# A two-layer graph transformer on one core: three tiles' q by rank kept on chip, row sums moved, and the last weight loads on another queue

## The chip, the cores and the metric

The kernel runs on one core of one Trainium2 chip. The time is the device time of one execution in microseconds. Of the kernel before there are three runs; their median is 1984.96 us (1980.67 to 1987.98). Besides, one execution was recorded by the hardware profiler.

TensorE (PE in the profile) multiplies matrices, VectorE (DVE), ScalarE (ACT) and GpSimd (POOL) work on rows, and SyncE (SP) only issues transfers. ScalarE and GpSimd issue transfers too. Each engine works through its own instructions in order; semaphores make one wait for another.

## The reference, cut to what matters

There are 2708 tokens of 512 numbers, 8 heads of 64, and two layers, each with its own weights. The graph is sparse: a token is joined to itself and to some others, at most 22 in the longest lists that the kernel plans for.

```
mask = adj + eye
q, k, v = h @ Wq.T + bq, h @ Wk.T + bk, h @ Wv.T + bv          # 8 heads of 64
scores = where(mask == 0, -1e9, q . k / sqrt(64))
ctx = softmax(scores) @ v
h1 = layer_norm(h + ctx @ Wo.T + bo, ln1)
h2 = layer_norm(h1 + relu(h1 @ W1.T + b1) @ W2.T + b2, ln2)     # W1: 2048 x 512
```

The second layer takes the first one's h2. Everything is float32.

## The kernel before, in words

`by_edges` works on edges. It sorts the tokens by the number of their neighbours ("by rank"), so that the 128 tokens of a tile have lists of about one length. There are 22 tiles; tile 21 has the shortest lists (3 entries at most) and only 20 tokens, tile 0 the longest (22). `order` is the order of work: tiles 21, 20, 19, 18, 8, 9, 7, 10 and so on, and two neighbours in it make a block (`blocks[0]` is 21 and 20, `blocks[1]` is 19 and 18).

**Keys and lists.** `first` projects k and v of all tokens in their given order and stores them in `kv_d` in DRAM; beside it VectorE reads the adjacency rows and finds each token's neighbours. `ranked` (line 735) then multiplies small matrices on TensorE (L742, L749), takes the ranks out of them on VectorE (L756 to L764), and GpSimd scatters each token's list to its rank (L768, 22 indirect transfers), reads all back (L779) and makes `ident_i`, the tokens in order of rank (L794). In the last two steps of the key phase `beside_keys` loads bias rows and the first weights; `load_second` adds two pairs of rows on VectorE (L1144), which stand in VectorE's order just ahead of L756.

**Queries.** `first_queries` (line 862) projects q of all tokens in their given order, two tiles at a time, into tiles `qs`, and stores them in `q_d` (`written`, L872 and L876). With tile t = `OWN` = 9 it begins on q by rank for the first four tiles of `order`: `own_rows` gathers the tokens' rows of x (two are asked for ahead of the loop, `xr`), `turned_own` transposes them on TensorE (L1100), `own_query` projects them. The first two q stay on chip. The other two are stored in `q_own` (L925) and loaded from there when attention asks for them (L971). All others are gathered from `q_d` by rank (L952), which can start when all of `q_d` is written.

**Attention.** `attend` is a generator. Each step takes one chunk of two list entries of a tile: GpSimd has gathered k and v of these neighbours (`loads`, L952, five buffers), VectorE multiplies by q (L991) and sums by head (L997), ScalarE takes exponentials (L1010) and weighs v (L1017), VectorE adds up (L1023, L1030). At the end of a tile `sums` and `divided` give the attended rows `cx` (L1061). `advance` takes steps as far as a credit allows, `through(k)` takes as many as block k needs. Attention's gathers of k, v and q stand on GpSimd's one queue.

**Feed-forward.** `attended` transposes `cx` (L1100, evicted at L1105), projects it by Wo (o, L568) and normalises (h, L1223 to L1094, with a reciprocal root on GpSimd, L1090). `turned` transposes h into `hT`. `feed_forward` (line 1240) runs over 16 slices f of W1: four matmuls `pf` (L1265), a relu on ScalarE (`ft`, L1273), and the second product `a` of three slices earlier (L1253). Three PSUM tiles hold `pf`, so that of slice f waits for the relu of slice f - 3. In the feed-forward of a block the next block's attention steps, its `attended` (at f = 10 and 11) and `turned` (after f = 15) are woven in.

For the first block `attended` is woven into the query loop: `beside_queries` (line 1417) transposes `cx` at t = NT - 7 = 15 and projects o at t = 16.

**Order.** TensorE, ScalarE and SyncE follow the order of the program. GpSimd does so up to the end of the query loop, VectorE in the query loop and at the start of layer 1; elsewhere a scheduler orders these two when the kernel is built.

**Weights.** W1 and W2 come in eight pieces each (`w1_0` to `w1_7`, `w2_0` to `w2_7`, 512 KB a piece). Pieces 5 to 7 lie in the buffers that the key and query loops use for x (`xg`) and for `kvs` and `qs`, so they can be loaded only after these loops. Lines 1439 to 1441 issue them on SyncE's queue behind the last stores of `q_d`:

```
for j in range(len(now.w1), NFC // 2):
    now.load_w1(j)
    now.load_w2(j)
```

Of the kernel before, what the change touches and what calls it, by code (L numbers as in the profile page):

```python
# [18 lines left out]
P = 128  # L19
DM = 512  # L20
# [22 lines left out]
XB, XBS = 256, 11  # L43
LEAD = 1.3
QT = 6
OWN = 9
EARLY = 3
PACE = (0.62, 0.72)

# [421 lines left out]
def by_edges(ctx: ExitStack, tc: tile.TileContext, x, xT, adj, layers, out, good):  # L471
# [30 lines left out]
    ps = ctx.enter_context(tc.tile_pool(name="ps", bufs=3, space=PSUM))  # L502

    own = {}
    at = None

    ident = const.tile([P, P], F32, name="ident")
# [10 lines left out]

    kv_d = [dram.tile([N, 2 * DM], F32, name=f"kv_d{n}") for n in range(NL)]
    q_d = [dram.tile([N, DM], F32, name=f"q_d{n}") for n in range(NL)]  # L520
    q_own = dram.tile([N, DM], F32, name="q_own")
# [340 lines left out]
    def first_queries(bq, wq, listed, pa, tokens, meanwhile):  # L862

        nonlocal at
        xrs = [own_rows(g) for g in blocks[0]]
        made = []

        def written():
            t, qs = made.pop(0)
            if t + 2 < NT:  # L870
                out = q_d[0][t * P : (t + 2) * P, :].rearrange("(two p) c -> p two c", p=P)
                nc.sync.dma_start(out=out, in_=qs)  # L872
                return
            for i in range(2):
                r = size(t + i)
                nc.sync.dma_start(out=q_d[0][(t + i) * P : (t + i) * P + r, :], in_=qs[:r, i])  # L876

        for t in range(NT):
            r = size(t)
            if t % 2 == 0 and made:  # L880
                written()
            q = project(tokens(t, 1), r, wq, "q", other=t % 2 > 0)
            if t % 2 == 0:
                qs = wts.tile([P, 2, DM], F32, tag=f"w2_{5 + t // 2 % 3}", name="qs")
                made.append((t, qs))
            nc.vector.scalar_tensor_tensor(
                qs[:r, t % 2], q[:r], DK**-0.5, bq[:r], ALU.mult, ALU.add
            )
            if t == OWN - 1:
                listed()  # L890
                pa.__exit__(None, None, None)
                at = ctx.enter_context(tc.tile_pool(name="at", bufs=2))
                for g in blocks[0]:
                    own[g] = at.tile([P, DM], F32, tag="q", name="q", bufs=QB)
                to = dict(own)
                next(ahead)
            if t in (OWN, OWN + 2):
                k = (t - OWN) // 2
                zTs = [turned_own(g, xr) for g, xr in zip(blocks[k], xrs)]
                for g, xr, zT in zip(blocks[k], xrs, zTs):  # L900
                    own_query(g, zT, to.get(g, xr), bq, wq)
                    advance(0.5)
                xrs = [own_rows(g) for g in blocks[1]] if k == 0 else []
            meanwhile(t)
        while made:
            written()

    def own_rows(g):
        r = size(g)
        xr = dn.tile([P, DM], F32, tag="row", name="xr", bufs=3)  # L910
        gather(xr[:r], x, ident_i[:r, g : g + 1])
        return xr
# [6 lines left out]
    def own_query(g, zT, to, bq, wq):  # L919

        r = size(g)
        q = project(lambda c: zT[:, c, :r], r, wq, "q")
        nc.vector.scalar_tensor_tensor(to[:r], q[:r], DK**-0.5, bq[:r], ALU.mult, ALU.add)
        if g in blocks[1]:
            nc.sync.dma_start(out=q_own[g * P : g * P + r, :], in_=to[:r])  # L925

    def checked():

# [32 lines left out]
    def asked(n, g):  # L961

        r = size(g)
        if g in own:
            return own.pop(g)
        q = at.tile([P, DM], F32, tag="q", name="q", bufs=QB)
        if n == 0 and g not in blocks[1]:
            gather(q[:r], q_d[0], ident_i[:r, g : g + 1])
        else:
            table = q_own if n == 0 else q_d[n]  # L970
            nc.sync.dma_start(out=q[:r], in_=table[g * P : g * P + r, :])  # L971
        return q

    def chunks_of(g):
# [134 lines left out]
    class Layer:  # L1109
# [27 lines left out]
        def load_second(self, part, temp):  # L1137

            w = self.w

            def sum_of(one, tag, other):
                t, u = row(w, one, tag), temp()
                nc.sync.dma_start(out=u, in_=other.to_broadcast([P, DM]))
                nc.vector.tensor_tensor(t, t, u, ALU.add)  # L1144
# [200 lines left out]
    def attend(n, got):  # L1345

        peak = small.tile([P, NT], F32, tag="peak", name="peak", bufs=1)
        nc.vector.memset(peak, 0.0)
        loaded = loads(n)
        steps = []  # L1350
        for g in order:
            cuts = chunks_of(g)
            steps += [(g, s0, c, i, i + 1 == len(cuts)) for i, (_, s0, c) in enumerate(cuts)]
            if g == order[1]:
                steps += [None] * 3
        steps += [None] * 3
        kv = next(loaded)
        yield 0.0
        q = asked(n, order[0])
        done = [None] * 3  # L1360
        for k, step in enumerate(steps):
            if step:
                g, s0, c, i, last = step
                if i == 0:
                    t = Tile(g, q)
                if k > 0:
                    kv = next(loaded)
                t.weights(kv, s0, c)
                if i == 1 and g != order[-1]:
                    q = asked(n, order[order.index(g) + 1])  # L1370
                done.append((t, kv, s0, c, last))
            else:
                done.append(None)
            t3, t2, t1 = done[-4:-1]
            if t1:
                t1[0].weigh(*t1[1:4])
            if t2 and t2[-1]:
                t2[0].sums(peak)
            if t3 and t3[-1]:
                got[t3[0].g] = t3[0].divided()  # L1380
# [22 lines left out]

    got = {}
    ahead = attend(0, got)
    early = {}

    def beside_keys(t):

        if t == NT - 5:  # L1410
            now.load_first()
        if t > NT - 3:
            now.load_second(t + 2 - NT, temp)
            now.load_w1(t + 2 - NT)
            now.load_w2(t + 2 - NT)

    def beside_queries(t):

        if len(now.w2) < 5:
            now.load_w1(len(now.w1), nc.scalar)  # L1420
            now.load_w2(len(now.w2), nc.scalar)
        if t > OWN:
            advance(1.0 if t < NT - 7 else 0.45)
        if t == NT - 7:
            through(0)
            early[0] = now.attended(blocks[0], got)
            next(early[0])
        if t == NT - 6:
            for _ in blocks[0]:
                next(early[0])  # L1430

# [3 lines left out]
    with tc.manual_schedule(engines={mybir.EngineType.Pool}):  # L1435
        made = first(layers[0], beside_keys)
        with tc.manual_schedule(engines={mybir.EngineType.DVE}):
            first_queries(*made, beside_queries)
    for j in range(len(now.w1), NFC // 2):
        now.load_w1(j)  # L1440
        now.load_w2(j)
    behind, pool = None, []
    for n in range(NL):
        last = n == NL - 1
# [23 lines left out]
        *_, hs = early[n]  # L1468
        hT = now.turned(blocks[0], hs)
        turning = projecting = None  # L1470
        for k, block in enumerate(blocks):
            more = k + 1 < NB
            asking = iter(())
# [2 lines left out]
            for f, zs in enumerate(now.feed_forward(block, hs, hT)):  # L1476
                if f == NFC:
                    break
                if f in (5, 6) and behind:
                    next(behind)  # L1480
                    if f == 6:
                        for _ in behind:
                            advance(1.0)
                        behind = None
                if more and f == 10:
                    through(k + 1)
                    projecting = now.attended(blocks[k + 1], got)
                    next(projecting)
                if more and f == 11:
                    for hs_next in projecting:  # L1490
                        advance(0.5 if k else 0.0)
                advance(PACE[n] if k else 1.1 if f < 10 else 0.4)
                if f in (0, 3, 7, 9):
                    next(asking, None)
                if more and f == NFC - 1:
                    finish(asking)
                    hT = now.turned(blocks[k + 1], hs_next)
                if n > 0 and (k, f) == (0, 2):
                    now.load_second(1, temp)
                if not last:  # L1500
# [14 lines left out]
                if not last and not more:  # L1515
# [7 lines left out]
                    if f == 7:  # L1523
                        finish(ahead)
                        pool += nxt.preloaded(order[:8], temp)
            if not last:
                behind = now.keys_values(block, zs)
            if more:
# [77 lines left out]
```

## Time and profile before

| | us |
|---|---|
| median of three runs | 1984.96 |
| lowest and highest run | 1980.67, 1987.98 |
| the profiled execution's own time | 1984.12 |
| its span, first to last instruction | 1982.0 |
| PE busy | 1903.5 |
| DVE busy | 1303.1 |
| ACT busy | 934.6 |
| POOL busy | 798.3 |

The mean clock granted to TensorE was 0.985 of full speed. In time: keys and lists until about 172, queries until 284 (with the first block's attention), the first block's feed-forward until 358, the rest of layer 0 until about 1184, layer 1 to the end.

A row of a timeline has the start in us, the duration in us, engine, line, operation, output and inputs by the program's names, the shapes, and how many instructions of one kind were joined; in brackets how long the engine had been idle before and what ended that. A float32 matmul is counted as two instructions. A row of the waits names engine, tile and line that waited, what it waited for, then the total in us, how often, and the longest.

### The profile page before, as it was taken

Reading aid. Unit: us, or ns where it says so; the run is one execution under the profiler, and the core shown is the slowest. Engines: PE = TensorE matmul, PEld = TensorE weight load, DVE = VectorE, ACT = ScalarE, POOL = GpSimd, SP = SyncE. Lnnn points to the kernel's source line nnn. Section 1 sums busy time; section 2 is a strip of 40 time slices with the busy share of each in tenths; the row PEclk is TensorE's granted clock in tenths of the full one; section 3 lists DMA queues with packets and bytes.
Section 4 is the critical chain, followed back from the end, with each engine's and each line's share of the span. In section 5 each row is a group of like instructions: output and inputs, shape, how many; then the busy total and the mean of one; then the engine's idle time right before and its main releaser. Section 6 shows DMA issues by size and latency. Waiting matters only on the chain. (4 is left out here: it accounts for less than half of the span.)

```text
span 1982.0 us, 20873 instructions
## 1 busy us (share of the span) xinstructions
PE 1903.5 (96%) x6162; PEld 1104.5 (56%) x6162; DVE 1303.1 (66%) x2140; ACT 934.6 (47%) x3219; POOL 798.3 (40%) x708
## 2 busy tenths in 40 slices
PE   8999888999999999999999997999999999999997
PEld 3443344565656556566566643556666566666664
DVE  6884478675957969568442025888587989777421
ACT  4660235464545646447441112665446765655320
POOL 3104436362634636435210023455356655544210
PEclk9999899999999999999999998999999999999998
DMA  8988658464745747455310746756465766554100
GB/s 321 357 296 293 191 200 296 154 208 143 227 154 174 236 150 246 154 173 176 133 58 22 225 157 225 258 182 212 155 208 186 244 205 225 177 188 151 42 11 13
DMA packets 131518, 367.96 MB, mean 186 GB/s; under 512 B 16701, under 2 KB 36525, under 8 KB 128687
## 3 DMA queue, kind: packets, MB, share of 16 engines
q0 software_dynamic: 69104, 246.35, 37.6%
q1 hardware_dynamic: 55780, 103.86, 15.3%
q10 hardware_dynamic: 6510, 16.34, 2.2%
q8 instruction: 50, 0.82, 0.2%
q14 instruction: 74, 0.60, 0.1%
HBM read 315.14 MB, written 51.35 MB: 185 GB/s over the span
## 5 line engine op out<-in xcount | busy, mean ns | idle before, releaser
L952 POOL DMA_INDIRECT kv<-kv_d,idx x420 | 547.0, 1302 | 494.0 <-DVE acc L1030 337.2
L1253 PE MATMUL a<-w,ft 128*128 128x512 f32 (+1 forms) x1408 | 665.3, 597 | 9.5 <-ACT ft L1273 9.5
L1265 PE MATMUL pf<-hT,w 128*128 128x256 f32 (+1 forms) x2816 | 638.2, 374 | 15.8 <-ACT ft L1273 8.0
L1265 PEld LDWEIGHTS pf<-hT,w 128*128 128x128 f32 x2816 | 523.2, 192 | 193.4 <-issue 107.7
L1253 PEld LDWEIGHTS a<-w,ft 128*128 128x128 f32 (+1 forms) x1408 | 255.9, 186 | 234.1 <-issue 198.3
L1273 ACT ACTIVATE ft<-pf,b 128x256 f32<-128x256 f32 (+1 forms) x352 | 157.9, 458 | 424.4 <-PE pf L1265 424.1
L991 DVE TENSOR_TENSOR kv<-kv,q 128x1024 f32<-128x1024 f32 (+3 forms) x222 | 256.5, 1158 | 144.6 <-DMA kv<-kv_d,idx 122.0
L1017 ACT ACTIVATE kv<-kv,p 128x64 f32<-128x64 f32 x1232 | 311.0, 335 | 5.0
L997 DVE TENSOR_REDUCE sc<-kv 128x16 f32<-128x1024 f32 (+3 forms) x222 | 254.6, 1153 | 1.0
L1030 DVE TENSOR_TENSOR acc<-acc,kv 128x1024 f32<-128x1024 f32 (+2 forms) x178 | 203.8, 1145 | 35.9 <-ACT kv L1017 35.4
L1090 POOL TENSOR_TENSOR rd<-va,mhalf 128x1 f32<-128x1 f32 (+1 forms) x88 | 85.7, 974 | 270.0 <-DVE va L1088 268.6
L1010 ACT ACTIVATE p<-sc,minus 128x8 f32<-128x8 f32 (+1 forms) x420 | 103.3, 295 | 190.3 <-DVE sc L997 189.9
L1023 DVE TENSOR_TENSOR kv<-kv,p 128x512 f32<-128x512 f32 (+1 forms) x178 | 121.5, 683 | 69.5 <-ACT p L1010 69.5
L568 PE MATMUL o<-wo,cT 128*128 128x512 f32 (+1 forms) x352 | 155.1, 593 | 0.5 <-ACT cT L1105 0.5
L568 PEld LDWEIGHTS o<-wo,cT 128*128 128x128 f32 (+1 forms) x352 | 65.1, 186 | 86.5 <-issue 75.8
L1061 ACT ACTIVATE cx<-acc,su 128x64 f32<-128x64 f32 (+1 forms) x352 | 88.5, 333 | 42.4 <-DVE su L1053 34.9
L1285 DVE TENSOR_TENSOR h<-a,h 128x512 f32<-128x512 f32 (+1 forms) x44 | 29.7, 677 | 106.0 <-PE a L1253 105.9
L1094 DVE SCALAR_TENSOR_TENSOR h<-h,rd,ln_b 128x512 f32<-128x512 f32 (+1 forms) x88 | 65.8, 748 | 48.1 <-POOL rd L1090 48.1
L660 ACT ACTIVATE code<-aj 128x2708 bf16<-128x2708 int32 (+1 forms) x22 | 73.3, 3330 | 48.1 <-POOL aj L656 41.2
L663 DVE MAX8 tops<-code 128x8 f32<-128x247 f32 (+2 forms) x242 | 82.8, 400 | 18.6 <-ACT code L660 18.5
L1017 ACT ACTIVATE acc<-kv,p 128x64 f32<-128x64 f32 (+1 forms) x352 | 88.8, 334 | 1.4
L568 PE MATMUL k<-wk,xg 128*128 128x512 f32 (+1 forms) x176 | 82.1, 611 | 6.8 <-DMA wk<-in_Wk 6.7
(132 smaller groups left out, 1466.3 us busy)
## 6 DMA issues: line engine op xcount, KB each, us to landing
aj<-in_adj SPq DMA_DIRECT2D x21, 1354.0 KB, 11.8
w<-in_W SPq DMA_DIRECT2D x26, 512.0 KB, 4.8
kv_d<-kvs ACTq DMA_DIRECT2D x21, 512.0 KB, 7.2
xg<-in_xT SPq DMA_DIRECT2D x20, 512.0 KB, 7.0
kv<-kv_d,idx POOLq DMA_INDIRECT x420, 5.6
q_d<-qs SPq DMA_DIRECT2D x22, 256.0 KB, 4.7
zT_d<-zT SPq DMA_DIRECT2D x22, 256.0 KB, 5.3
xb_d<-h SPq DMA_DIRECT2D x21, 256.0 KB, 5.3
```

The lines of the kernel that those rows point to most:

```text
L568: nc.tensor.matmul(o[:r], xs(c), wm[:, c, :], start=(c == 0), stop=(c == NC - 1))
L952: nc.gpsimd.indirect_dma_start(out=to, out_offset=None, in_=table[:, :], in_offset=bass.IndirectOffsetOnAxis(ap=s, axis=0), bounds_check=N ...
L991: nc.vector.tensor_tensor(kv[:r, :c, :DM], kv[:r, :c, :DM], self.q[:r].unsqueeze(1).to_broadcast([r, c, DM]), ALU.mult,)
L997: nc.vector.tensor_reduce(self.sc[:r, s0 : s0 + c, :], kv[:r, :c, :DM].rearrange("p s (h d) -> p s h d", d=DK), AX.X, ALU.add,)
L1010: nc.scalar.activation(p[:r, s, :], self.sc[:r, s, :], AF.Exp, bias=minus[:r, g, s : s + 1])
L1017: nc.scalar.activation(to[:, i, hd], kv[:r, i, DM + h * DK : DM + (h + 1) * DK], AF.Copy, scale=p[:r, s0 + i, h : h + 1],)
L1023: nc.vector.tensor_tensor(to[:, 0, :].rearrange("p (h d) -> p h d", d=DK), kv[:r, 0, DM:].rearrange("p (h d) -> p h d", d=DK), p[:r, s0, : ...
L1030: nc.vector.tensor_tensor(self.acc[:r, :c, :], self.acc[:r, :c, :], kv[:r, :c, DM:], ALU.add)
L1061: nc.scalar.activation(cx[:r, hd], self.acc[:r, 0, hd], AF.Copy, scale=self.su[:r, h : h + 1])
L1253: nc.tensor.matmul(a[:r], fts[f][:, c0 : c0 + r], self.w2[f // 2][:, f % 2, :], start=(f == 0), stop=(f == NFC - 1),)
L1265: nc.tensor.matmul(pf[:, :w], self.w1[f // 2][:, c, f % 2 * P : f % 2 * P + P], hT[:, c, :w], start=(c == 0), stop=(c == NC - 1),)
L1273: nc.scalar.activation(ft[:, :w], pf[:, :w], AF.Relu, bias=self.b1[:, f : f + 1])
```

## The change

- `OWN` is 10, and q by rank is made for three tiles instead of four: the rows of `order[:3]` (tiles 21, 20, 19) are gathered together and transposed together at t = 10; the first two are projected there, the third at t = 12. All three stay on chip. `q_own` is gone.
- Tile 18 and all later ones get q from `q_d` by rank. `asked` returns nothing until all of `q_d` is written in the program, and `attend` then asks again.
- The two sums of bias rows are put in a list and taken at t = 3 of the query loop.
- In the query loop, `cx` of the first block is transposed at t = NT - 6 = 16 and o is projected at t = 17; the pace of attention around it differs. In the first block's feed-forward the next block's `attended` comes at f = 11 and 12.
- Pieces 5 to 7 of W1 and W2 are issued from ScalarE's queue at f = 0, 2 and 4 of the first block.
- GpSimd follows the order of the program in the first block of layer 0 too.

```diff
-OWN = 9
+OWN = 10
...
-        xrs = [own_rows(g) for g in blocks[0]]
+        xrs = [own_rows(g) for g in order[:3]]
...
-                for g in blocks[0]:
+                for g in order[:3]:
                     own[g] = at.tile([P, DM], F32, tag="q", name="q", bufs=QB)
...
-            if t in (OWN, OWN + 2):
-                k = (t - OWN) // 2
-                zTs = [turned_own(g, xr) for g, xr in zip(blocks[k], xrs)]
-                for g, xr, zT in zip(blocks[k], xrs, zTs):
-                    own_query(g, zT, to.get(g, xr), bq, wq)
+            if t == OWN:
+                zTs = [turned_own(g, xr) for g, xr in zip(order, xrs)]
+                for g, zT in zip(blocks[0], zTs):
+                    own_query(g, zT, to[g], bq, wq)
                     advance(0.5)
-                xrs = [own_rows(g) for g in blocks[1]] if k == 0 else []
+            if t == OWN + 2:
+                own_query(order[2], zTs[2], to[order[2]], bq, wq)
             meanwhile(t)
         while made:
             written()
+        all_made.append(True)
...
-        if g in blocks[1]:
-            nc.sync.dma_start(out=q_own[g * P : g * P + r, :], in_=to[:r])
...
+        if n == 0 and not all_made:
+            return None
         q = at.tile([P, DM], F32, tag="q", name="q", bufs=QB)
-        if n == 0 and g not in blocks[1]:
-            gather(q[:r], q_d[0], ident_i[:r, g : g + 1])
-        else:
-            table = q_own if n == 0 else q_d[n]
-            nc.sync.dma_start(out=q[:r], in_=table[g * P : g * P + r, :])
+        fetch(n, q, q_d[n], g)
         return q
...
-                nc.vector.tensor_tensor(t, t, u, ALU.add)
+                if later is None:
+                    nc.vector.tensor_tensor(t, t, u, ALU.add)
+                else:
+                    later.append((t, u))
...
-                    t = Tile(g, q)
+                    while q is None:
+                        q = asked(n, g)
+                        if q is None:
+                            yield None
+                    t, q = Tile(g, q), None
...
-                if i == 1 and g != order[-1]:
+                if i > 0 and q is None and g != order[-1]:
                     q = asked(n, order[order.index(g) + 1])
...
-            now.load_second(t + 2 - NT, temp)
+            now.load_second(t + 2 - NT, temp, sums)
...
+        if t == 3:
+            for total, other in sums:
+                nc.vector.tensor_tensor(total, total, other, ALU.add)
...
-            advance(1.0 if t < NT - 7 else 0.45)
-        if t == NT - 7:
+            advance(1.0 if t < NT - 6 else 0.6)
+        if t == NT - 6:
             through(0)
             early[0] = now.attended(blocks[0], got)
             next(early[0])
-        if t == NT - 6:
+        if t == NT - 5:
             for _ in blocks[0]:
                 next(early[0])
...
-    for j in range(len(now.w1), NFC // 2):
-        now.load_w1(j)
-        now.load_w2(j)
...
+        in_order = ExitStack()
+        if n == 0:
+            in_order.enter_context(tc.manual_schedule(engines={mybir.EngineType.Pool}))
         for k, block in enumerate(blocks):
...
-                if more and f == 10:
+                if more and f == 10 + (k + n == 0):
...
-                if more and f == 11:
+                if more and f == 11 + (k + n == 0):
...
-                advance(PACE[n] if k else 1.1 if f < 10 else 0.4)
+                advance(PACE[n] if k else 1.1 if f < 11 else 0.4)
...
+                if k == 0 and len(now.w1) < NFC // 2 and f % 2 == 0:
+                    now.load_w1(len(now.w1), nc.scalar)
+                    now.load_w2(len(now.w2), nc.scalar)
...
+            in_order.close()
```

More of the change, by code (lines that the diff above doesn't have):

```diff
@@ L504, in by_edges @@
     own = {}
+    all_made = []
     at = None
@@ L520, in by_edges @@
     q_d = [dram.tile([N, DM], F32, name=f"q_d{n}") for n in range(NL)]
-    q_own = dram.tile([N, DM], F32, name="q_own")
     zT_d = [None] + [dram.tile([NT, P, NC, P], F32, name=f"zT_d{n}") for n in range(1, NL)]
@@ L1135, in load_w2, with load_second @@
             self.w2.append(t)
-        def load_second(self, part, temp):
+        def load_second(self, part, temp, later=None):
             w = self.w
@@ L1405, in by_edges @@
     ahead = attend(0, got)
-    early = {}
+    early, sums = {}, []
     def beside_keys(t):
```

## The prediction

> **What bounds the kernel now.** I read the page first (engine totals, then slices), then who TensorE waited for, then the timelines of each engine where those waits lie.
>
> ```profile
> span 1982.0 us, 20873 instructions
> PE 1903.5 (96%) x6162; PEld 1104.5 (56%) x6162; DVE 1303.1 (66%) x2140; ACT 934.6 (47%) x3219; POOL 798.3 (40%) x708
> ```
>
> TensorE (PE) works 96% of the span, in an order written by hand. So the end moves by what is taken out of PE's order plus what its idle time shrinks, as long as nothing later stops it. The waits of PE in the first 345 us, the part that the change rewrites (total, times, longest):
>
> ```profile
> PE tp L1100 <- DMA xr<-in_x,ident_i: 9.3, 2, 6.8
> PE pf L1265 <- ACT ft L1273: 6.8, 2, 4.8
> PE k L568 <- DMA wk<-in_Wk: 6.7, 1, 6.7
> PE pf L1265 <- ACT hT L1105: 5.2, 1, 5.2
> PE pr L742 <- DVE kvs L838: 4.5, 1, 4.5
> ```
>
> Rows one, two and four (21 us) belong to the edited steps; the other two stay. The first hole, in order of time (start, duration, idle before):
>
> ```profile
> 168.11 0.69 DVE L1144 TENSOR_TENSOR ln_b<-ln_b,temp 128x512 f32<-128x512 f32 x1 [2.37 <-DMA temp<-in_bo]
> 213.55 0.58 PE L1100 MATMUL tp<-ident,xr 20*128 20x20 f32 x4 [6.79 <-DMA xr<-in_x,ident_i]
> 216.68 1.09 PE L1100 MATMUL tp<-ident,xr 128*128 128x128 f32 x4 [2.55 <-DMA xr<-in_x,ident_i]
> 217.69 8.66 PE L568 MATMUL q<-wq,zT 128*20 128x512 f32 x16
> 234.34 7.13 PE L568 MATMUL q<-wq,zT 128*128 128x512 f32 x16 [0.24 <-ACT zT L1102]
> ```
>
> A sum of two bias rows sits on VectorE ahead of the ranks and waits for its load; behind it come ranks, 22 scatters, the read back, and the gather that PE waits for. After the wait PE runs 16 matmul passes in 8.66 us that otherwise take 7.1. The second hole, in the first feed-forward block:
>
> ```profile
> 294.21 0.67 DVE L886 SCALAR_TENSOR_TENSOR qs<-q,bq 20x512 f32<-20x512 f32 x1
> 299.71 2.46 POOL L952 DMA_INDIRECT q<-q_d,ident_i  x1 [0.30 <-issue]
> 307.34 1.22 DVE L991 TENSOR_TENSOR kv<-kv,q 128x1024 f32<-128x1024 f32 x1 [5.93 <-issue]
> 310.33 0.49 ACT L1010 ACTIVATE p<-sc,minus 128x8 f32<-128x8 f32 x2 [6.99 <-DVE sc L997]
> 313.20 2.34 PE L1265 MATMUL pf<-hT,w 128*128 128x148 f32 x8 [4.84 <-ACT ft L1273]
> 319.88 1.27 PE L1265 MATMUL pf<-hT,w 128*128 128x148 f32 x8 [1.99 <-ACT ft L1273]
> ```
>
> The last q row leaves VectorE at 294.9, is stored, gathered by rank, multiplied at 307.3 (12.5 us later); ScalarE's next exponential waits for it, and the relu (ft) behind that in ScalarE's order holds PE.
>
> **The change, part by part** (times on the clock of this execution).
>
> *Row sums moved behind the fourth q.* Without the two sums, VectorE's last rank step follows PE's second rank product (ends 167.96) by 0.96 us of listed work: ranks at 168.9 instead of 170.4, so gathers land 1.5 earlier. The sums (2 x 0.69) go where VectorE idles 2.74 us per q tile; were that idle time gone, they would cost 1.4.
>
> *One tile later, three own tiles.* PE does 11 instead of 10 q tiles first (34.60 for ten, so 3.44 more work before the wait): until 210.0. The first gather is there at 213.55 - 1.5 = 212.05, the second at 215.2, a third 1.3 behind it (spacing of GpSimd's issues). Waits 2.05 + 2.6 + 0.4 = 5.05 instead of 9.34: 4.3 saved. All three flips (0.5, 0.9, 0.9) end at 217.4.
>
> [...] The row says that the own queries after this hole take 8.5 us (217.69 to 226.19). [...] I take 7.0 (saves 1.5) and keep the row for the range.
>
> *Fourth own query dropped.* PE loses one flip (0.52), one projection (3.43) and the 0.24 wait for it: 4.2. Two stores of q_own and two loads go too; VectorE waited 6.85 us at 261 for the late one, so tile 19's attention now starts with its q on chip.
>
> So far 4.3 + 1.5 + 4.2 = **10.0 us** at the last own query: 234.75 with 13 q tiles done, against 241.31 with 12. The attended tile comes 12.4 us behind that query's eviction (242.2 to 254.56 now), thus at 247.9; PE needs it at 248.5: no new wait, but only 0.6 of cover.
>
> *Block start.* Projections and the remaining q tiles are the same work, so the flip of h moves from 283.95 to 274.0. The hT wait of 5.2 came from ScalarE's order: an exponential ahead of hT waited for VectorE until 286.87, because q_own was late. That score is now ready at about 259. Flip to first pf then takes 2.5 instead of 6.4, and four pf's at full clock 4.4 instead of 6.8: PE is through its first accumulation at 282.8 (before: 299.1).
>
> *All q's for tile 18 and on by rank.* This is the new wait. The last q row is evicted at 274.75 (PE's end, nothing ahead on VectorE). The store lands in 3.2 to 5.5 us (the two sizes traced), the gather in 3.4, 4.6 or 7.5:
>
> ```profile
> L952 POOL DMA_INDIRECT q<-q_d,ident_i x18: 1001/1012/2459, 299.7 to 870.4; - x18
> DMA to landing us min/median/max: 3.4/4.6/7.5
> ```
>
> With 4.35 and 4.6, q lands at 283.8. On VectorE a small scaling of bo stands ahead; its load, now issued by SyncE straight after the q stores, lands in 6.8 (row of its like), with one accumulation behind it: 284.1. Two products and a sum (3.6), exponentials and weighing (2.45), relu (0.37): PE's fifth pf starts at 290.5, a 7.7 us wait that before lay later (4.84). Behind the waiting exponential on ScalarE stand this ft and the first weight load. From there ScalarE's order, as the changed kernel has it, paces PE: four more weighings (2.45 each), one exponential (0.28), two divisions (1.95 each), four relus (0.33 each) and a wait of 1.4 for VectorE's sums ahead of the second division: 16.7 us to the relu that frees the ninth pf, **307.2 instead of 319.88: 12.7 us ahead**. The half clock after the wait (1.5 by row 313.20) lies inside that pacing and costs nothing.
>
> *Last weights on ScalarE's queue.* Six loads of 512 KB leave SyncE and follow relus 0, 2, 4. Their issue costs ScalarE nothing: the wk load issued at 334.75 (0.37) lay inside eight copies that took 2.01 as always. They land in 8 to 13 us and are used some 20 us after their issue; with that gone, each us of lateness costs one. Now they burst just before the q gather (409 GB/s at 300 to 304); spreading them is why I take the median gather and not 7.5.
>
> *GpSimd in program order, flips of block 1 one step later.* The reciprocal roots stand behind gathers whose buffers come free earlier than the roots are due. The h flip of block 1 gets one step (3.03) less cover: 352.4 against h at 349.03 leaves 0.4. I charge 0.5, bounds 0 to 2.
>
> Sum: 12.7 - 0.5 = **12.2, say 12**, on the execution's 1984.12 (span 1982.0 and 2.1 around it): 1972.1. The median of the runs shown, 1984.96, is 0.84 above it: **1973.0**, -0.6%.
>
> **Rivals.**
> (a) *The q round trip stays as long as now*, 12.5 us instead of 9.35. For: it is the same path. Against: DMA engines were saturated then (share 1.05 at 308 to 312), with weights in front. Gain 12 - 3.1: 1976.1.
> (b) *Attention doesn't follow.* If its engines stay where they are, PE meets the next flips of cx early: they ran at 407.41 with cx ready at 401.2, so only 6.2 is kept: 1978.8. For: 32 waits of VectorE on kv gathers, 122 us in all. Against: VectorE and ScalarE idle between 345 and 500 and their order follows PE's.
> (c) *Faster*: store 3.2, gather 3.4, bo early: 2.6 sooner, 1970.4; with shorter VectorE waits behind it (the 1.4) 1969.
> (d) *Slower*: the same round trip, at the fifth pf, price 1 us per us. From 21.4 us between eviction and product nothing is gained; from 31 the kernel is 0.5% slower. Store and gather at their longest make 13, so 5%.
> (e) *The sums don't shorten the rank chain* (a scatter bound elsewhere): 1.5 less, 1974.5; inside the likeliest case's range, as is the half clock.
>
> **How the numbers follow.** Likeliest 0.58 (own range 1969.5 to 1976, nearly all below 1975.0), (c) 0.15, (a) 0.12, (b) 0.10, (d) 0.05. About 0.5% (9.9 us) is what a measurement of this kernel can tell from no change, since three runs of one kernel spread 7.3 us. Faster: most of the likeliest and all of (c), a little of (a): 0.73. Same: the rest of the likeliest, (a), (b): 0.22. Slower 0.05. The range goes from (c) less half the runs' spread to (b) plus some of it: 1966.5 to 1980.5.
>
> **What would show it.** Ranks near 169; the first xr flip after some 2 us of idle, own queries at full clock; last own query near 235; pf's start near 276.5 without a wait for hT; then one wait of PE on ft of 6 to 9 us, and the first cx flip of block 1 near 320. Wrong: an ft wait above 12 us, a wait for hT in block 1, or waits on cx after 345 that grow by what was won.

## The result and the profile after

The changed kernel took a median of 1973.76 us (8 runs, 1969.27 to 1979.97), the kernel before beside it 1983.62 (8 runs). The ratio is 0.9956, 95% interval 0.994 to 0.9972. Measured once more, unedited, beside the last experiments, it took 1977.95 (14 runs) against 1982.95: 0.9974, 0.9962 to 0.9986. So the change wins 5 to 9 us, where the forecast was 12.

The head of the changed kernel's page (span; busy time of TensorE):

```profile
span 1972.6 us, 20843 instructions
PE 1898.6 (96%) x6150; PEld 1101.4 (56%) x6150; DVE 1303.4 (66%) x2139; ACT 933.0 (47%) x3218; POOL 793.1 (40%) x708
```

Its span is 9.4 us shorter, 4.9 of it less busy time on TensorE and 4.5 less idle time. That these add up to something near the forecast hides a larger gain and a larger loss. TensorE's timeline of the changed kernel (start, duration, what ended the idle time before it):

```profile
209.02 0.58 PE L1097 MATMUL tp<-ident,xr 20*128 20x20 f32 x4 [2.81 <-DMA xr<-in_x,ident_i]
...
212.65 8.65 PE L568 MATMUL q<-wq,zT 128*20 128x512 f32 x16
...
270.65 1.01 PE L1097 MATMUL tp<-ident,h 20*128 20x20 f32 x8
272.20 4.31 PE L1265 MATMUL pf<-hT,w 128*128 128x148 f32 x32 [0.54 <-ACT hT L1102]
284.76 2.34 PE L1265 MATMUL pf<-hT,w 128*128 128x148 f32 x8 [6.22 <-ACT ft L1273]
301.31 1.27 PE L1265 MATMUL pf<-hT,w 128*128 128x148 f32 x8 [1.38 <-ACT ft L1273]
...
335.49 0.66 PE L1097 MATMUL tp<-ident,h 128*128 128x128 f32 x4 [1.51 <-DVE h L1091]
...
378.17 5.98 PE L568 MATMUL v<-wv,zT 128*128 128x512 f32 x8 [5.17 <-DVE kvs L1316]
...
422.71 1.04 PE L1097 MATMUL tp<-ident,h 128*128 128x128 f32 x8
```

and three rows of the kernel before that belong beside the last ones:

```profile
351.95 1.04 PE L1100 MATMUL tp<-ident,h 128*128 128x128 f32 x8
...
390.10 3.70 PE L568 MATMUL v<-wv,zT 128*128 128x512 f32 x8 [0.27 <-DVE kvs L1316]
...
432.37 1.04 PE L1100 MATMUL tp<-ident,h 128*128 128x128 f32 x8
```

There are two halves to see. Down to 301.31 (319.88 before) the waits of the edited steps have shrunk: 18.6 us ahead, of which 4.0 come from an earlier start of the queries and not from the edits (next paragraph). In the row at 378.17 TensorE waits 5.17 us for VectorE, where the kernel before waited 0.27 (390.10), and then runs its eight passes in 5.98 instead of 3.70. This is the projection of layer 1's keys and values, woven into the second feed-forward block, which the change doesn't touch.

One more thing has to be taken out before traces are compared. The first q tile started at 172.16 in the profile of before and at 168.18 in that of after. Of these 3.98 us, 3.0 are an earlier rank product (161.10 instead of 164.10), which waits for VectorE at the end of the key phase. In the twelve other profiles of this study, of either kernel's variants, the first q tile starts between 165.45 and 170.65, with no relation to the edits that I can see (the mean is 170.4 over the three profiles of the old order and 169.1 over the eleven of the new one, so a share of 1 us isn't excluded); the profile shown ahead of the prediction had the latest of all. I therefore count every trace from its first q tile. "Lead" below is how much earlier than in the kernel before a flip of h comes, so counted: of the first block (283.95 before), of the second (351.95) and of the third (432.37). Worked out for the changed kernel: its first q tile is 3.98 earlier; 283.95 - 270.65 - 3.98 = 9.3, 351.95 - 333.38 - 3.98 = 14.6, 432.37 - 422.71 - 3.98 = 5.7.

| kernel | first q tile | lead, first block | second | third | ratio to the kernel before (95%) |
|---|---|---|---|---|---|
| changed | 168.18 | 9.3 | 14.6 | 5.7 | 0.9956 (0.994 to 0.9972) |
| changed, again | 169.03 | 9.3 | 14.8 | 3.1 | 0.9974 (0.9962 to 0.9986) |
| keys and values later | 169.58 | 8.8 | 12.6 | 1.5 | 0.9979 (0.9964 to 0.9993) |
| the same on the kernel before | 168.39 | 0.7 | 0.7 | 0.5 | 1.0008 (1.0 to 1.0015) |
| row sums back | 170.22 | 9.1 | 14.4 | 5.8 | 0.9968 (0.9956 to 0.9981) |
| last weights back | 169.70 | 9.1 | 6.8 | -1.0 | 0.9996 (0.9987 to 1.0005) |
| only the weights moved | 170.52 | 0.7 | 2.7 | -1.8 | 1.0001 (0.9989 to 1.0012) |
| GpSimd by the scheduler | 170.65 | 11.5 | 13.2 | 11.1 | 0.9942 (0.9927 to 0.9957) |
| fourth own query again | 169.80 | 4.4 | 2.3 | -5.1 | 1.0021 (1.0007 to 1.0035) |
| own queries a tile later | 165.45 | 7.3 | 11.2 | 3.1 | 0.9958 (0.9943 to 0.9974) |
| program order to the flips | 168.83 | 9.4 | 15.0 | 11.0 | 0.9947 (0.9928 to 0.9966) |
| the same, weights later | 169.26 | 8.8 | 10.0 | 10.4 | 0.9942 (0.992 to 0.9963) |
| flips of cx back | 169.78 | 8.7 | 12.6 | 7.3 | 0.9952 (0.9935 to 0.9969) |

Each lead is read from one profile, each ratio from many runs. The lead at the third block agrees with the gain by ratio within 3 us (0.001 of ratio is 2 us), but for the own queries a tile later, where it is 5 off. The changed kernel has 15 us of lead at the second block and gives 9 to 12 of them back inside it. The experiments ask what makes the 15, and where the 9 to 12 go.

### The profile page after: what moved, and what is told of

Its sections match the earlier page's. It is cut to its first block, busy times and chain, and to the rows that moved or that the text cites. A ratio compares the mean times of both kernels' runs of the same rounds, so it can differ in the third digit from the quotient of the medians.

```text
span 1972.6 us, 20843 instructions
## 1 busy us (share of the span) xinstructions
PE 1898.6 (96%) x6150; PEld 1101.4 (56%) x6150; DVE 1303.4 (66%) x2139; ACT 933.0 (47%) x3218; POOL 793.1 (40%) x708
## 3 DMA queue, kind: packets, MB, share of 16 engines
q1 hardware_dynamic: 52804, 99.66, 14.8%
## 5 line engine op out<-in xcount | busy, mean ns | idle before, releaser
L1285 DVE TENSOR_TENSOR h<-a,h 128x512 f32<-128x512 f32 (+1 forms) x44 | 29.7, 676 | 106.0 <-PE a L1253 105.8
L1324 POOL DMA_INDIRECT kv_d<-kvs,ident_i x22 | 23.2, 1053 | 163.6 <-ACT kvs L1318 88.2
```

## The experiments

### Where the loss is: keys and values later

My first theory was the place of one instruction. VectorE's eviction of the projected keys (L1316) stands in its order behind attention steps, and these were waiting for their gathers.

```
-                if f in (5, 6) and behind:
+                late = 3 * (k + n == 1)
+                if f in (5 + late, 6 + late) and behind:
                     next(behind)
-                    if f == 6:
+                    if f == 6 + late:
```

> The changed kernel with one edit: in the second feed-forward block the first tile's layer-1 keys and values are projected at chunks 8 and 9 instead of 5 and 6. Theory T (the lead is lost because the eviction of kvs stands in VectorE's order behind attention steps that wait for their gathers): the wait of PE v on kvs (5.17) and the half-clocked passes behind it (5.98 instead of 3.70) go, the lead over the kernel before at that point stays near 16 instead of 9.7, and the time falls by 6 to 7 us against the changed kernel, to about 0.992 of the kernel before. Rival R1 (that wait was chance of one execution): it need not show in either place, and the time stays within 1.5 us of the changed kernel, 0.9955. Rival R2 (the gathers that VectorE waits for bound the lead anyway): the wait goes, but another of 5 to 7 us comes up later, at the attended tile of a block or at layer 1's first query (wait on qs 10.6 now, 16 to 17 then), and the time stays at 0.9955.

> The kernel before with the same one edit (keys and values of the first tile at chunks 8 and 9 of the second block). Theory T: TensorE waited only 0.27 us for kvs there before, so nothing is to be had: ratio 1.000, within 1 us. If the later place were better in itself, whatever the lead, this kernel would gain as much as the changed one does, 6 to 7 us.

Measured: 0.9979 and 1.0008. The theory fell: no time was won, and the wait didn't go, it grew (in a profiled execution that was one of the two slowest of six, 1984.1 us against a median of 1977.45). TensorE's row in the changed kernel with this edit:

```profile
393.93 6.16 PE L568 MATMUL v<-wv,zT 128*128 128x512 f32 x8 [8.42 <-DVE kvs L1316]
```

Three chunks later VectorE is still late, again behind products that wait for gathers of kv (4.75, 3.93 and 4.49 us each). So it isn't this instruction's place: attention as a whole has not followed TensorE into the second block, and what it waits for is GpSimd's gathers. Counted over the same work, from the second block's flip of h to the third's, VectorE waited 16.7 us for kv in both kernels (7 waits each): the second block's gathers are not slower, they are not earlier. The changed kernel's extra waits lie in the first block, from its flip of h to the second's: 8.3 us (3 waits) instead of 1.0 (2). The product that waits longest ahead of the keys stood at 365.79 in the changed kernel and at 375.59 in the kernel before. Counted as the leads are, that is 5.8 us of lead, where TensorE had come with 14.6.

### Row sums and weights, each put back

```
-            now.load_second(t + 2 - NT, temp, sums)
+            now.load_second(t + 2 - NT, temp)
```

> The changed kernel with the two row sums back on VectorE in the key phase, ahead of the ranks. Theory T, by my steps: the ranks come 1.5 us later behind the rank product (0.9 to 2.5), the three waits for xr go from 3.8 to about 5.3, the first block's ninth pf is 1.5 later, and the time is up by 1.5 at most, 0.9963, hardly to be told from 0.9955. The end of the key phase (rank product at 161.10 after, 164.10 before): by T chance of an execution, so anywhere from 160 to 165; by the rival that the sums or their loads hold the key phase it is 3 us later here, at 164, and the time is 4 to 5 us up.

Measured: 0.9968, between the two measurements of the changed kernel. From the rank product to the ranks it is 6.39 us (163.09 to 169.48), as in the kernel before (6.34), against 4.58 in the changed one: the sums do cost the 1.8 us. But the three waits for xr were 3.8 in both. Here the tables scattered by rank came back 9.5 us after the last scatter was issued, against 10.8 in the changed kernel's profile, which hides 1.3 of the 1.8. Whether the 1.8 us ever reach the end stays open. The key phase doesn't depend on the sums: the first q tile (170.22) lies among the others.

The weights back on SyncE, behind the q stores as in the kernel before:

```
+    for j in range(len(now.w1), NFC // 2):
+        now.load_w1(j)
+        now.load_w2(j)
     behind, pool = None, []
...
-                if k == 0 and len(now.w1) < NFC // 2 and f % 2 == 0:
-                    now.load_w1(len(now.w1), nc.scalar)
-                    now.load_w2(len(now.w2), nc.scalar)
```

> The changed kernel with the last six weight loads back on SyncE, all behind the q stores. Theory T: the trip of q from its eviction to its product stays at 7.6 us (7 to 9), the wait on ft at the fifth pf near 6.2, and the time within 1 us of the changed kernel. Rival W (the trip is short because these 3 MB no longer cross it): the trip is 10 to 12.5 us, the wait on ft 9 to 11, the ninth pf 3 to 5 us later, and the time 3 to 5 us up.

Measured: 0.9996. Nearly the whole gain is gone, 4 us against the changed kernel's second measurement and 8 against its first. Its timeline (VectorE's last q row, the next product, TensorE's fifth pf):

```profile
272.53 0.68 DVE L886 SCALAR_TENSOR_TENSOR qs<-q,bq 20x512 f32<-20x512 f32 x1 [0.21 <-PE q L568]
...
283.78 2.36 DVE L988 TENSOR_TENSOR kv<-kv,q 128x1024 f32<-128x1024 f32 x2 [4.41 <-DMA q<-q_d,ident_i]
...
290.17 2.34 PE L1265 MATMUL pf<-hT,w 128*128 128x148 f32 x8 [9.87 <-ACT ft L1273]
```

and the same of the changed kernel:

```profile
270.76 0.68 DVE L886 SCALAR_TENSOR_TENSOR qs<-q,bq 20x512 f32<-20x512 f32 x1 [0.21 <-PE q L568]
274.93 1.00 POOL L951 DMA_INDIRECT q<-q_d,ident_i  x1 [7.89 <-DMA bk<-in_bk]
278.37 2.36 DVE L988 TENSOR_TENSOR kv<-kv,q 128x1024 f32<-128x1024 f32 x2 [0.77 <-DMA q<-q_d,ident_i]
```

From the end of the eviction to the product: 283.78 - 273.21 = 10.6 us with the weights in front, 278.37 - 271.44 = 6.9 without. The gather was issued as soon in both (276.61 and 274.93, 3.4 and 3.5 us behind the eviction), so what grew is its own trip to the product, from 3.4 to 7.2. VectorE waits 4.41 for q instead of 0.77, and TensorE's wait on ft is 3.65 longer. The late q is not all: the next four chunks take 18.8 us instead of 16.55, the stretch from there to the second block's flip 33.7 instead of 32.1, and the lead at that flip is 6.8 instead of 14.6. VectorE's waits for kv in this block sum to 11.6 us instead of 8.3. Rival W is right in its mechanism; it had put the cost at 3 to 5 us.

The weights alone, on the kernel before:

> The kernel before with one edit: its last six weight loads leave SyncE, where they all stand behind the q stores and ahead of the q gathers, and are issued by ScalarE behind relus 0, 2 and 4 of the first feed-forward block. My prediction costed this move at nothing (at most a q gather at its median instead of its longest): ratio 0.999 to 1.000. Rival W (these loads fill the DMA engines ahead of the q gather and the first gathers of kv): the trip of q from its eviction to its product falls from 12.5 to 9 or 10 us, the wait on ft behind it from 4.84 to about 2, and what follows it in that block loses its late gathers too: 3 to 6 us less, ratio 0.997 to 0.9985. If the move alone carries the change, it is 0.9956.

Measured: 1.0001. The trip of q falls from 12.5 to 10.5, TensorE's two waits on ft from 6.8 to 5.5 in sum, the lead at the second block is 2.7, and at the third it is gone. So the same move is worth nothing by itself and 4 to 8 us inside the change. Why is not shown: q by rank was already waited for in the kernel before, and the 2.7 us were won there too. In this trace TensorE gives lead back at the keys and values (a wait of 1.96 for kvs and 5.40 for the passes, instead of 0.27 and 3.70), with GpSimd ordered by the scheduler.

### GpSimd's program order

```
         if n == 0:
-            in_order.enter_context(tc.manual_schedule(engines={mybir.EngineType.Pool}))
+            pass
```

> The changed kernel without the program order of GpSimd in the first layer's blocks (the scheduler places its instructions again). My prediction: that order brings and costs nothing, so the same within 1 us, 0.9956. Rival P (it carries part of the gain): the scheduler puts three gathers of kv ahead of tile 18's q, at 1.3 us each and more where one waits for its buffer; the trip of q goes from 7 to 10 or 12 us, the wait on ft from 6.2 to 9 or 11, and 3 to 5 us are lost: 0.998. Rival P2 (it costs: a gather at 334.8 stands behind a reciprocal root that waits for VectorE, in the kernel before the gather goes first): 1 to 3 us faster than the changed kernel.

Measured: 0.9942. Rival P2 is right: the second block loses only 2.1 us of lead (13.2 to 11.1) instead of 9 to 12. Of rival P a part of the delay came, but not by its mechanism. The trip of q is 9.1 us instead of 6.9 and the wait on ft 8.35 instead of 6.22, but no gather of kv holds q up: only one more stands ahead of it, and it ended 6.5 us before q's gather (277.43). That gather was issued 5.7 us behind the eviction instead of 3.5, when a transfer landed, and took 3.4 to the product as in the changed kernel. Why the transfer came later is open; it is one profile. The next trial keeps the order where q was thought to need it and ends it at the flip of cx:

```
+                if f == 10 + (k + n == 0):
+                    in_order.close()
                 if more and f == 10 + (k + n == 0):
```

> The changed kernel itself, unedited, on the same chip as the next three and against the same runs of the kernel before: 0.9956, within 0.0015, if the difference measured first holds; the end of the key phase (rank product) anywhere from 160 to 165, whatever the kernel.

> The changed kernel with GpSimd's program order ended at the step of the first block in which the second block's cx is flipped (chunk 11), and not with the block. Theory P2 (program order costs because a gather of kv stands behind reciprocal roots that wait for VectorE): early q as in the changed kernel, so 15.6 us of lead at the second block's first flip beyond the shift of the key phase, and in the second block only some 2 us of it lost, as without any program order, instead of 8.8: 3 to 5 us faster than the changed kernel, 0.993 to 0.994. If the second block loses its 8.8 all the same, the gain without program order came from elsewhere, and the time is that of the changed kernel.

Measured: 0.9974 for the control, 0.9947 for this one: 0.27% or 5.4 us, with an uncertainty of about 4.5 (the two intervals overlap by a little); against the changed kernel's first measurement, 0.9956, nothing could be told. The traces say it more sharply, because the two are alike up to the second block's flip (leads 14.8 and 15.0) and 8 us apart at the third (3.1 and 11.0). Its flip of h there, control first:

```profile
426.14 1.04 PE L1097 MATMUL tp<-ident,h 128*128 128x128 f32 x8
```

```profile
418.04 1.04 PE L1097 MATMUL tp<-ident,h 128*128 128x128 f32 x8
```

GpSimd's rows of the control:

```profile
326.78 1.42 POOL L951 DMA_INDIRECT kv<-kv_d,idx  x1 [0.30 <-issue]
328.51 1.00 POOL L951 DMA_INDIRECT xb<-in_x,ident_i  x1 [0.30 <-issue]
329.54 0.63 POOL L1087 TENSOR_TENSOR rd<-va,mhalf 128x1 f32<-128x1 f32 x1
330.62 1.30 POOL L951 DMA_INDIRECT xb<-in_x,ident_i  x1 [0.46 <-DVE h L1223]
334.36 1.60 POOL L1087 TENSOR_TENSOR rd<-va,mhalf 128x1 f32<-128x1 f32 x1 [2.43 <-DVE va L1085]
336.14 1.52 POOL L951 DMA_INDIRECT kv<-kv_d,idx  x1 [0.18 <-ACT hT L1102]
```

and of the kernel whose program order ends at the flips:

```profile
325.22 1.42 POOL L951 DMA_INDIRECT kv<-kv_d,idx  x1 [0.30 <-issue]
326.95 0.99 POOL L951 DMA_INDIRECT kv<-kv_d,idx  x1 [0.30 <-issue]
327.96 0.63 POOL L1087 TENSOR_TENSOR rd<-va,mhalf 128x1 f32<-128x1 f32 x1
328.78 1.56 POOL L951 DMA_INDIRECT kv<-kv_d,idx  x1 [0.18 <-issue]
```

In program order the next gather of kv (336.14) stands behind two gathers of xb and both reciprocal roots that normalise the second block's h, woven into the first block, and the second root (334.36) waits for VectorE's variance. The scheduler issues that gather at 326.95, 9.2 us earlier (the gather ahead of it 1.6), and the next at 328.78, in traces that lie 0.4 us apart at the second block's first flip. The product that waits longest ahead of the keys follows: 367.54 in the control, 361.89 here. Then TensorE's two rows at the keys and values, control first, read 6.50 us of wait and 6.76 of work against 1.84 and 3.70:

```profile
380.81 6.76 PE L568 MATMUL v<-wv,zT 128*128 128x512 f32 x8 [6.50 <-DVE kvs L1316]
```

```profile
375.77 3.70 PE L568 MATMUL v<-wv,zT 128*128 128x512 f32 x8 [1.84 <-DVE kvs L1316]
```

The other profiles agree. Between the second and the third flip the eight profiles of the changed kernel and its variants with GpSimd in program order to the block's end lose 5.3 to 11.7 us of lead, the three without it from nothing to 4.0 (and the kernel before with the weights moved, which the scheduler orders, 4.5). That the order of GpSimd from the flips on makes most of the loss is shown. That the roots are the culprits among what it moves (gathers of xb and of q move too) is read from the rows. Whether the order ahead of the flips helps is not shown: with it or without it the time is the same (0.9947 and 0.9942).

One more step, the last weights issued behind relus 4, 6 and 8:

```
-                if k == 0 and len(now.w1) < NFC // 2 and f % 2 == 0:
+                if k == 0 and len(now.w1) < NFC // 2 and f in (4, 6, 8):
```

> As the kernel with GpSimd's program order ended at the flip of cx, and the last six weight loads two by two behind relus 4, 6 and 8 instead of 0, 2 and 4. If these loads still hold up gathers at 282 to 300 us (VectorE waits 1.0, 4.2 and 3.1 there for kv), those waits shrink by some 3 and 1 to 3 us are won: 0.992 to 0.993. If the DMA engines are as full later, the waits only move: the same. Slower if a load lands behind the chunk that uses it (chunks 10, 12, 14): each us late costs one.

Measured: 0.9942, no different from 0.9947. The lead at the second block is smaller (10.0) and at the third it is the same (10.4). VectorE's waits for kv in the first block sum to 9.1 us, against 8.5: in that stretch the waits only move. With a median of 1970.9, 1971.4 and 1971.7 us, this kernel, the one before it and the one with GpSimd left to the scheduler all beat the kernel before by 10 to 12 us, and the changed kernel by 2 to 7, as one takes its first or second measurement; among the three nothing can be told.

### Own queries and flips

The fourth own query made again:

```
             if t == OWN + 2:
-                own_query(order[2], zTs[2], to[order[2]], bq, wq)
+                zTs.append(turned_own(order[3], xrs[0]))
+                for g, zT in zip(blocks[1], zTs[2:]):
+                    own_query(g, zT, to.get(g, xrs[0]), bq, wq)
+                    advance(0.5)
...
+        if n == 0 and g == order[3]:
+            nc.sync.dma_start(out=q[:r], in_=q_own[g * P : g * P + r, :])
+            return q
```

> The changed kernel with the fourth own query made again (flip, projection, store, and a load in place of tile 18's gather by rank); all else as changed. Theory T, by my steps: TensorE pays 4.2 us for it (0.52 + 3.43 + 0.24), so the flip of h stands 4 later; tile 18's q is then there early, the wait on ft of 6.2 at the fifth pf and the half-clocked passes behind it go, and the next tile's q, by rank, comes late instead, at about the place where the kernel before waited (4.84 at 313). Sum between +4 (the wait comes back for the next tile) and -3 (it doesn't): 0.9956 to 0.9975, or 0.994.

Measured: 1.0021, slower than the kernel before and 9 to 13 us behind the changed one. The expectation missed its size. The added flip and projection take 3.9 us of TensorE in this trace, where 4.2 was worked out; the lead at the first block falls by 4.9, in which a wait of 2.40 for x, one of 2.00 for h and shorter waits for xr are mixed. The rest is the load of that q. Rows of VectorE and TensorE:

```profile
261.22 1.22 DVE L998 TENSOR_TENSOR kv<-kv,q 128x1024 f32<-128x1024 f32 x1 [10.84 <-DMA q<-q_own]
...
284.56 6.73 PE L1275 MATMUL pf<-hT,w 128*128 128x148 f32 x32 [5.21 <-ACT hT L1112]
```

This q was stored at 236.68, but SyncE issued its load only at 249.90, behind two stores of q and two loads of x. VectorE waits 10.84 us; ScalarE's next exponential waits for VectorE, the copy of hT stands behind it, and TensorE's wait of 5.21 for hT is back, to a hundredth as it was before the change. So bringing back the round trip of one tile's q undoes the whole gain, as bringing back the place of the weights does nearly: the two parts don't add up, and without either one next to nothing is left of the gain.

The own queries one q tile later (OWN 11 instead of 10):

> The changed kernel with the own queries one q tile later (behind twelve tiles instead of eleven). Theory T: the waits for xr (2.81, 0.53, 0.42) go altogether, 3.8 us; if idle time is what halves the clock of the two own queries behind them, they run at full clock, 7.1 instead of 8.65; if transposes count as idle time too, the three flips alone (some 3 us) leave them at 8 or more. The attended tile comes 3.4 later against TensorE's order, but q tiles that stood behind the own queries now stand ahead: the first flip of cx (245.27, its cx ready about then) waits 3 to 5 us, and that takes the gain back: the time within 1.5 us of the changed kernel. Rival (TensorE's order decides, attention follows): 4 to 5 us less, 0.9935.

Measured: 0.9958, as the changed kernel. All waits for xr went, and the first flip of cx waited 1.67. In this profile an unrelated wait of 2.64 us for x fell into the q tiles, so its leads say little. What it shows is the clock:

```profile
211.19 1.45 PE L1097 MATMUL tp<-ident,xr 20*128 20x20 f32 x12
212.56 7.24 PE L568 MATMUL q<-wq,zT 128*20 128x512 f32 x16
```

Behind flips without idle time the pair of own queries runs at full clock: 7.24 against 8.65. (The projection of o at 249.64 of the changed kernel, 16 passes too, took 7.24 at a granted clock of 1.00.) It did too with GpSimd left to the scheduler, where the two waits were 0.85 and 1.60, but not behind one wait of 2.8. In the eight profiles whose first wait for xr was 2.66 to 2.94, the pair took 8.61 to 9.35. In the changed kernel the clock granted to TensorE was 0.95 of full speed over 206 to 209 us and 0.50 over 209 to 212.65, so it fell in that first wait, ahead of the flips; flips alone didn't lower it (with the own queries later the pair took its 7.24 straight behind twelve flip passes, 1.45 us), and between 209.02 and 212.65 they didn't bring it back.

The flips of cx one chunk earlier again:

```
-                if more and f == 10 + (k + n == 0):
+                if more and f == 10:
...
-                if more and f == 11 + (k + n == 0):
+                if more and f == 11:
```

> The changed kernel with the second block's cx flipped one chunk earlier again, as in the kernel before. My prediction charged the later flip 0.5 us (0 to 2), in the wait for h at the second block's start (1.5 measured). Here that wait goes; in its place cx may be late, for its row sums reach ScalarE when they did: a wait on cx of up to 3. Between 1.5 faster and 2 slower than the changed kernel: 0.995 to 0.9966.

Measured: 0.9952 against the control's 0.9974, with intervals that overlap: 0 to 8 us faster than the changed kernel, so moving the flips later is not shown to be a gain. The wait for h at the second block (2.2 in the control, 1.5 in the first profile) is gone here, and at 353.44 TensorE waits 2.17 for VectorE's last sum of the first block (L1285) instead. What of this reaches the end is not settled.

## Why the prediction was right and wrong

The time fell inside the range. That the first median, 1973.76, lies at the predicted 1973.0 is luck: the kernel before ran at 1983.62 beside it and not at 1984.96, the second median is 1977.95, and a lead that was larger than predicted was followed by a loss that the sum didn't contain. Against the kernel before the gain is 5.2 to 8.7 us by ratio (0.26% and 0.44%), not 12: less than the 0.5% that I had called the bound of what can be told, where I gave 0.73 to more than that.

- **Sums moved.** Sized 1.5, measured 1.8 at the ranks. The rival that it doesn't reach TensorE isn't excluded.
- **Waits for xr.** Sized 5.05, measured 3.76 and 3.81. Mechanism right; 1.3 too much. (The sum itself slipped by 0.2: 172.16 + 34.60 + 3.44 is 210.2 and not 210.0, which makes 4.85.)
- **Clock of the own queries.** I took 7.0 over the row's 8.5, and the row was right: 8.65 and not 7.0, behind one wait of 2.81. No run shows the 7.0, and the 1.5 that it puts into the sum, behind waits like these: in the eight profiles with a first wait for xr of 2.66 to 2.94 the pair took 8.61 to 9.35, and 7.24 only where no wait for xr was above 1.60. The row of before that comes nearest to 7.0 at full clock (16 passes in 7.13, at 234.34) stands behind a wait of 0.24. That step was wrong by 1.6, about what the one before it was too dear.
- **Fourth own query.** 4.2 sized, 3.9 in the trace that brings it back, and the hT wait of 5.2 hangs on it as the step said. Lead at the first block 9.3, where 283.95 - 274.0 = 9.95 was predicted.
- **The new wait on ft.** There, at the fifth pf, where it was put: 6.2 instead of 7.7, since the trip of q took 6.9 and not 9.35, both transfers near their shortest (gather issued 3.5 behind the eviction, product 3.4 behind that). At the ninth pf the lead is 14.6, and 14.8 in the control, where 12.7 was predicted.
- **Weights on ScalarE's queue.** I priced their issue at nothing and let their spreading decide between a median and a long gather, 2.9 us. The runs show 4 to 8 us for it inside the change. This term was mis-sized: 3 MB in front of the gathers lengthen the trip of q by 3.6 us and VectorE's waits for kv in that block by 3.3.
- **GpSimd in program order.** This step failed. It said that the roots stand behind gathers whose buffers come free earlier, and cost the move at nothing. It never asked what stands behind the roots: a gather of kv, issued 9.2 us later than without the order. That is worth 8 us of lead at the third block (3.1 against 11.0) and 5.4 us of time, give or take 4.5.
- **Rival (b), attention doesn't follow**, had the price nearly right (6.2 us kept; 5.7 and 3.1 of lead measured, 5.2 to 8.7 of time) and the place wrong. I looked for it at the waits on cx after 400; it came at the eviction of the keys at 378, which I hadn't looked at, because TensorE had waited 0.27 there.

So the likeliest case described TensorE's first block well, and rival (b) what came of it in the second. What happened is both.

## What to carry to other kernels

An order given to an engine is meant for one instruction and also fixes all those behind it: go through the queue past each waiting instruction (here the reciprocal roots), and end the order where its purpose ends. Time won on the bottleneck engine has to be followed until the engines that feed it have won it too; a wait of a quarter of a microsecond ahead of a gain of fifteen is where the gain will be met. Here the bulk loads with time to spare belonged behind the gather that TensorE waited for, but the move was worth nothing alone and 4 to 8 us inside the change: parts of a change need not add up, so take each out of the whole as well as trying it alone.

## What the runs showed of the hardware

In the changed kernel the clock granted to TensorE was 0.50 of full speed over 378.17 to 381, in the row behind the wait of 5.17 us, and 1.00 again over 384 to 386. The halved clock doesn't follow from the length of the idle time alone. In all fourteen profiles I took the rows of five or more passes of 128x512 that start behind at least 1.2 us of idle TensorE (without the first row of each profile), 119 rows. Behind 1.92 us or less, all 53 ran at full clock; behind 3.3 us or more, all 29 were slowed; behind 1.96 to 3.21 us, 16 were full and 21 slowed. Eight passes take 3.70 us at full clock and 5.2 to 6.8 when slowed, most often 5.40. The row at 1189.93 of the changed kernel came behind 3.04 us and took 3.70, at a granted clock of 1.00; a row at 718.94 with the fourth own query came behind 1.98 and took 5.40.

The counts show no more than these three groups; what decides between 1.96 and 3.21 us is not shown. For a forecast in this kernel, as an estimate from these rows: a new wait below 1.9 us costs its length, one above 3.3 costs 1.5 to 3 us more (5.2 to 6.8 for eight passes instead of 3.70), and in between it can go either way.
